# A graph layer on one core: gathered rows of two tables in separate buffers, and the order of a few steps around the start of the pair loop

## The chip, the cores and the metric

The kernel runs on one core of a Trainium2 chip. The metric is the device time of one execution in microseconds (us); the time before is the median of 9 runs. The profile comes from one further execution. In the text, PE is TensorE (PEld its weight loads), DVE is VectorE, ACT is ScalarE, POOL is GpSimd and SP is SyncE. L492 means line 492 of the kernel before.

## The reference, cut to what matters

```python
# 6250 nodes of 128 values, 100000 edges (src, dst) sorted by dst; hidden width 256
h = relu(concat(x[src], x[dst]) @ Wm1 + bm1)     # [100000, 256]
h = relu(h @ Wm2 + bm2)                          # [100000, 256]
messages = h @ Wm3 + bm3
agg = segment_sum(messages, dst) / clip(count_of_edges(dst), 1.0)
upd = relu(concat(x, agg) @ Wn1 + bn1) @ Wn2 + bn2
out = layernorm(x + (x + upd))                   # [6250, 128]
```

## The kernel before

**Two tables first.** The first product is split: `concat(x[src], x[dst]) @ Wm1` is a row of `A = x @ Wm1[:128]` plus a row of `B = x @ Wm1[128:]`. A prologue turns x by 13 blocks of 512 nodes (`turn`), multiplies (`products`, L258) and writes table A in float32 (`a_table`) and table B as three bfloat16 terms whose sum is the float32 value (`b_table`) to DRAM. B is computed five blocks behind A. Meanwhile small loads fetch weights (`weights`, whose loads are held back until a certain block is turned by a one-element VectorE copy into their targets), and the edges' indices are arranged: `srcT` holds the source of every edge, one column of 128 edges for each gather; `pbase`, `dloc` and `tilei` say to which window of 21 destinations each tile of 128 edges belongs.

The prologue also computes `x @ Wn1[:128]` into the space of x and of its transpose (`xu`): `x_part(b, ...)` does it for block b, two matmuls (L355) and two evacuations (L358 on ACT, L360 on DVE). Ten blocks are done in the prologue, block 9 (`X_FIRST`) after the first `first_layer`, block 10 at the end of the loop.

**The pair loop.** Edges go in groups of 512 (four tiles of 128), two groups to a pair, 98 pairs, written as a Python loop (L644) and so unrolled. The order of PE, DVE, ACT and POOL inside it is the order of the program text. One turn of the loop holds, for different pairs:

- `fetch` for the pair ahead: on POOL eight indirect DMAs (L492), each of which brings 128 rows of A (1 KB each) by the indices in `srcT`; on SP eight loads of 64 rows of B's terms (L498). All go into one tile `rows` of five parts, four for A and one, reread as bfloat16, for B; there are two such buffers, so the gathers of a pair wait for the first layer of the pair two before it.
- `destinations` for the pair ahead (L384, issued by ACT): the edges' destinations, spread over 64 partitions.
- `turned` and `add_up` for the pair three back: 12 transposes on PE (L584) into two banks, then eight small additions on DVE (L594) into the running sums `acc`.
- `make_hot`: DVE compares destinations with node numbers, giving the one-hot matrices `oht` (L516) and `oh` (L519).
- `first_layer`: on PE 32 transposes of A's rows (L533) into the PSUM tile `ph`, then 16 matmuls that add B's rows through `oht` (L540); on ACT four evacuations with bias and ReLU into `h1` (L546).
- `sums` for the pair two back: 16 matmul instructions (L565) into two banks, copied out by ACT (L573).
- `second_layer` for the pair before: 32 matmul instructions (L555) into four banks, evacuated by four DVE operations with the maximum against minus the bias (L557) into `h2s`.

`bank()` hands out four PSUM banks in turn, so a turn of the loop goes twice round the four: `turned` takes two, `sums` two, `second_layer` four. `turned` of the next turn therefore waits for the first two L557, and the third and fourth bank of `second_layer` wait for the two copies L573. The wait of POOL's first gather is for the last L540, because L540 is the last reader of the shared `rows` tile; before it, POOL also waits for the eight SP loads that last wrote that buffer.

```python
rows = ld.tile([P, 2, (GT + 1) * H], F32, name="rows", bufs=2)      # L487
ag = rows[:, i, :GT * H].rearrange("p (j h) -> p j h", j=GT)        # A's rows, L490
bw = rows[:, i, GT * H:].bitcast(BF16).rearrange(...)               # B's terms, L495
```

**After the loop** come a loop for windows that are too wide (its count is computed from the data), and the node stage over 15 stretches of nodes: mean of the messages, update, layer norm, store.

Of the kernel before, what the change touches and what calls it, by code (L numbers as in the profile page):

```python
# [27 lines left out]
def kernel(  # L28
# [121 lines left out]
    with tc.tile_pool(name="prep", bufs=1) as prep, tc.tile_pool(  # L150
# [34 lines left out]
            nc.gpsimd.dma_start(bu1, bn1.rearrange("(c p) -> p c", p=P))  # L185

        def weights(block):
            for t in (wu1, w3, w2):
                nc.vector.tensor_copy(t[:, 0, :1], xT[:, block * 4 * P:block * 4 * P + 1])
            nc.gpsimd.dma_start(nb2[:, 0, :], bm2.rearrange("(o h) -> o h", o=1).to_broadcast([P, H]))  # L190
            nc.sync.dma_start(wu1, wn1.rearrange("(k p) h -> p k h", p=P))
            nc.sync.dma_start(w3, wm3.rearrange("(k p) h -> p k h", p=P))
            nc.sync.dma_start(w2, wm2.rearrange("(k p) h -> p k h", p=P))

        nc.vector.memset(xT[:, N:], 0.0)

# [77 lines left out]
        def b_stores():  # L274
            while due:
                nc.sync.dma_start(*due.pop(0))
# [71 lines left out]
        def x_part(b, bank, engines):  # L348


            n0, n1 = 4 * b * P, min(4 * b * P + 4 * P, N)
            for c, eng in zip((1, 0), engines):
                pxu = bank().rearrange("p t h -> p (t h)")[:, :n1 - n0]
                i = 4 if b < BLOCKS - 1 else 1
                nc.tensor.matmul(pxu.rearrange("p (n i) -> p i n", i=i), wu1[:, 0, c * P:(c + 1) * P],  # L355
                                 xT[:, n0:n1].rearrange("p (i n) -> p i n", i=i), start=True, stop=True)
                if eng is nc.scalar:
                    nc.scalar.activation(xu[c][:, n0:n1], pxu, AF.Identity, bias=bu1[:, c:c + 1])  # L358
                else:
                    nc.vector.tensor_scalar(xu[c][:, n0:n1], pxu, bu1[:, c:c + 1], None, op0=ALU.add)  # L360
                yield

        def whole(steps):
            for _ in steps:
                pass
# [9 lines left out]
        def destinations(g, ng, dst_row):  # L375

            db = ld.tile([P, 2, 2 * P], I32, name="db", bufs=3)
            if isinstance(g, int) and g < 6:

                nc.vector.tensor_copy(db[:, 0, :1], srcT[:, 0, :1])  # L380
            for h in range(2):
                edges = dst_row[:, ds(g * GE, ng * GE)].rearrange("o (s e) -> o s e", s=ng)
                edges = edges[:, :, h * 2 * P:(h + 1) * 2 * P]
                nc.scalar.dma_start(db[h * NQ:(h + 1) * NQ, :ng, :], edges.to_broadcast([NQ, ng, 2 * P]))  # L384
            return [db[:, k, :] for k in range(ng)]
# [20 lines left out]
        for i in range(BLOCKS):  # L406
            if i in X_LOADS:
                load_x(*X_LOADS[i], behind=i)
                if X_LOADS[i][1] == BLOCKS - 1:
                    nc.sync.dma_start(x_sb[:N - NTF * P, NTF, :], x[NTF * P:, :])  # L410
            for n, t0 in enumerate(range(4 * i, min(4 * i + 4, NT), 2)):

                if n == (i == 0) and i + 1 < BLOCKS:
                    turn(4 * i + 4)
                a_table(t0)
            b_stores()
            for _ in range(min(len(blank), 3 if i < BEHIND else 1)):
                nc.gpsimd.memset(blank.pop(0), 0.0)
            if i == BEHIND + 1:
                weights(i)  # L420
            if i == INDICES:
                starts()
            if i - INDICES in (1, 2):
                columns(i - INDICES - 1)
                partition_bases(i - INDICES - 1)
            if i == BLOCKS - 1:
                nc.scalar.copy(tilei, base[0:1].rearrange("p r w -> p (r w)"))
                nc.gpsimd.tensor_scalar(nb2, nb2, -1.0, None, op0=ALU.mult)
            if i >= BEHIND:
                b_block(i - BEHIND)  # L430
            if BLOCKS - 3 <= i:
                early.append(destinations(2 * len(early), 2, dst_row))
        assert not blank
        behind = list(X_BEHIND)
        with tc.manual_schedule(engines={ENG.DVE}):
            for n, j in enumerate(range(BLOCKS - BEHIND, BLOCKS)):
                if n < 4:
                    whole(x_part(behind.pop(0), bank_pb, (nc.scalar, (nc.scalar, nc.vector)[n % 2])))
                b_block(j)
                b_stores()  # L440
            b_terms()
            b_stores()
        stores.close()


        turns.enter_context(tc.manual_schedule(engines={ENG.DVE}))
        for n, b in enumerate(behind):
            whole(x_part(b, bank_pb, (nc.vector if n >= len(behind) - 2 else nc.scalar, nc.vector)))
        pb3 = pp.tile([P, 1], F32, name="pb3", tag="pp")
        for c in range(HC):  # L450
            nc.tensor.matmul(pb3, w3[:, c, :], b2[:, c:c + 1], start=(c == 0), stop=(c == HC - 1))
        nc.vector.tensor_add(b23, b3, pb3)

# [10 lines left out]
    with edge, tc.tile_pool(name="wk", bufs=2) as wk, tc.tile_pool(  # L464
# [19 lines left out]
        def fetch(groups, queues):  # L484


            rows = ld.tile([P, 2, (GT + 1) * H], F32, name="rows", bufs=2)  # L487
            got = []
            for i, ((idx, firsts), queue) in enumerate(zip(groups, queues)):
                ag = rows[:, i, :GT * H].rearrange("p (j h) -> p j h", j=GT)  # L490
                for j in range(GT):
                    nc.gpsimd.indirect_dma_start(  # L492
                        out=ag[:, j, :], out_offset=None, in_=atab[:, :],
                        in_offset=bass.IndirectOffsetOnAxis(ap=idx[:, j:j + 1], axis=0))
                bw = rows[:, i, GT * H:].bitcast(BF16).rearrange("p (k h) -> p k h", k=2)  # L495
                for j, first in enumerate(firsts):
                    terms = btab[ds(first, WB + 1)].rearrange("n c h -> (n c) h")
                    queue.dma_start(bw[j // 2 * NQ:(j // 2 + 1) * NQ, j % 2, :], terms[:NQ])  # L498
                got.append((ag, bw))
            return got  # L500
# [23 lines left out]

        halves = [slice(h * NQ, (h + 1) * NQ) for h in range(2)]

        def first_layer(got, ohts, nts):
            ph = p1.tile([P, 2, 2, HC, 2 * P], F32, name="ph")
            for i, ((ag, bw), nt) in enumerate(zip(got, nts)):
                for c in range(HC):  # L530
                    for u in range(GT):
                        for h in range(nt // 2):
                            nc.tensor.matmul(ph[:, i, h, c, u * NQ:(u + 1) * NQ], ag[halves[h], u, c * P:(c + 1) * P],  # L533
                                             ident[halves[h], halves[h]], is_transpose=True,
                                             start=(c == 0 and u == 0), stop=False, skip_group_check=True)
            for i, ((ag, bw), nt) in enumerate(zip(got, nts)):
                for c in range(HC):
                    for k in range(2):
                        for h in range(nt // 2):
                            nc.tensor.matmul(ph[:, i, h, c, k * P:(k + 1) * P], bw[halves[h], k, c * P:(c + 1) * P],  # L540
                                             ohts[halves[h], i, k, :], start=False, stop=True, skip_group_check=True)
            h1 = wk.tile([P, 2, HC, GE], F32, name="h1")
            for i in reversed(range(len(nts))):
                nh = nts[i] // 2
                for c in range(HC):
                    nc.scalar.activation(h1[:, i, c, :nh * 2 * P].rearrange("p (h e) -> p h e", h=nh),  # L546
                                         ph[:, i, :nh, c, :], AF.Relu, bias=b1[:, c:c + 1])
            return h1

        def second_layer(h1, h2, nt):  # L550
# [93 lines left out]
        for i in range(NP + 4):  # L644
# [28 lines left out]
                    double((i - after) // 4, step)  # L673
            if p + 1 < NP:
                make_hot(p + 1)
            if p == 0:
                clear(3)
            if p < NP:
                s = st[p]
                s["h1"] = first_layer(s.pop("got"), s.pop("ohts"), s["nts"])  # L680
            if p == 0:
                whole(x_part(X_FIRST, bank, (nc.scalar, nc.vector)))
            if p - 2 == NP - 1:
                next(rest)
            if 0 <= p - 2 < NP:
# [269 lines left out]
```

## Time and profile before

| | |
|---|---|
| median of 9 runs | 1709.92 us (1701.01 to 1717.09) |
| the profiled execution: its own time, its span | 1717.37 us, 1715.2 us |
| mean granted clock of TensorE | 0.855 |
| busy: PE, PEld | 1343.8 us (78%), 1056.1 us |
| busy: DVE, ACT, POOL | 658.5, 380.6, 812.0 us |
| prologue, up to the first L533 | 87.8 us |
| pair loop, up to the node stage | from 87.8 to about 1642 us |
| node stage | about 73 us |
| window 400 to 1200 us | PE busy 617.3 of 800 us, POOL 381.7, DVE 282.3, ACT 148.6 |

The profile's page gives busy time by engine and by line; the waits say who stood for whom; the timeline gives single instructions in order. Matmuls are pipelined and their ends are modelled, so PE's busy share is an upper bound of its work. "remote" as the releaser of a wait means that the profile has no instruction that ended just then.

### The profile page before, as it was taken

The page shows a single profiled execution, that of the slowest core. Times are in us where ns is not written, and L with a number is a line of the kernel's source. Part 1 is how long each engine was busy: PE and PEld are TensorE (multiplying, and loading weights), DVE is VectorE, ACT ScalarE, POOL GpSimd, SP SyncE. Part 2 cuts the span into 40 slices and gives each one's busy share as a digit, 9 for nine tenths or more (in the row PEclk, how much of TensorE's full clock was granted, in tenths as well). Part 3 has the DMA queues.
Part 4 walks back from the last instruction along what each step waited for, and adds up shares of the span by engine and source line. Part 5 has one row for each costly group of instructions (what it writes and reads, how often), then busy time and mean ns, then how long its engine had stood idle before and what let it go on. Part 6 is the DMA issues. An engine that isn't in the chain of part 4 may idle for free. (4 is left out here: it accounts for less than half of the span.)

```text
span 1715.2 us, 32176 instructions
## 1 busy us (share of the span) xinstructions
PE 1343.8 (78%) x11222; PEld 1056.1 (62%) x11223; DVE 658.5 (38%) x2073; ACT 380.6 (22%) x768; POOL 812.0 (47%) x871
## 2 busy tenths in 40 slices
PE   9868778777777777777877877777788787777898
PEld 8456566566665655656656665666666566656656
DVE  5534323333332333333333333333233333333467
ACT  6512112212211211212211221221222122212235
POOL 7654454445445445445544544544544454445121
PEclk9888888888888888788888888878888888888899
DMA  8743344334334334334434433433433333333133
GB/s 295 271 117 110 98 111 113 105 104 117 106 99 123 106 94 122 105 93 123 116 87 114 114 89 101 111 88 98 110 99 98 102 107 101 98 103 108 38 111 111
DMA packets 167752, 193.67 MB, mean 113 GB/s; under 512 B 31074, under 2 KB 133428, under 8 KB 167572
## 3 DMA queue, kind: packets, MB, share of 16 engines
q0 software_dynamic: 38160, 103.75, 21.9%
q1 hardware_dynamic: 100640, 61.84, 12.3%
q10 hardware_dynamic: 28788, 26.01, 5.3%
q8 instruction: 89, 1.46, 0.4%
q14 instruction: 75, 0.61, 0.1%
HBM read 168.97 MB, written 22.88 MB: 112 GB/s over the span
## 5 line engine op out<-in xcount | busy, mean ns | idle before, releaser
L492 POOL DMA_INDIRECT rows<-atab,srcT x784 | 748.4, 955 | 800.0 <-PE ph L540 581.7
L555 PE MATMUL bank<-w,h 128*128 128x256 f32 x3128 | 710.5, 386 | 0.6 <-issue 0.4
L555 PEld LDWEIGHTS bank<-w,h 128*128 128x128 f32 x3128 | 593.8, 193 | 136.4 <-PE bank L565 57.9
L557 DVE TENSOR_TENSOR h<-bank,nb 128x512 f32<-128x512 f32 x391 | 254.8, 688 | 967.3 <-remote 474.4
L546 ACT ACTIVATE h<-ph,b 128x512 f32<-128x512 f32 x392 | 237.0, 688 | 1244.3 <-PE ph L540 1206.4
L584 PE MATMUL bank<-ident,part 64*128 64x64 f32 x1173 | 102.3, 289 | 328.8 <-DVE h L557 317.8
L584 PEld LDWEIGHTS bank<-ident,part 64*128 64x128 f32 x1173 | 73.0, 183 | 375.8 <-DVE h L557 338.3
L533 PE MATMUL ph<-ident,rows 64*128 64x64 f32 x3128 | 191.3, 300 | 15.8 <-issue 14.3
L533 PEld LDWEIGHTS ph<-ident,rows 64*128 64x128 f32 x3128 | 178.6, 209 | 19.6 <-issue 16.1
L594 DVE TENSOR_TENSOR acc<-acc,bank 128x63 f32 x782 | 171.7, 220 | 34.8 <-DVE acc L594 2.1
L565 PE MATMUL bank<-h,oh 128*32 128x257 f32 x1564 | 156.2, 536 | 0.2 <-ACT x_sb L358 0.2
L540 PE MATMUL ph<-oht,rows 64*128 64x128 bf16 x1564 | 110.2, 304 | 6.3 <-issue 5.5
L540 PEld LDWEIGHTS <-rows 64*128 64x128 bf16 x1564 | 94.3, 144 | 7.2 <-issue 7.2
L516 DVE TENSOR_SCALAR oht<-db,pbase 128x128 bf16<-128x128 int32 x392 | 94.8, 288 | 0.3
L565 PEld LDWEIGHTS bank<-h,oh 128*32 128x32 f32 x1564 | 52.3, 143 | 57.0 <-issue 29.5
L573 ACT COPY part<-bank 128x257 f32<-128x257 f32 x196 | 66.6, 400 | 11.9 <-PE bank L565 9.0
L519 DVE TENSOR_TENSOR oh<-iota_n,dloc 128x128 f32<-128x128 f32 x196 | 55.4, 283 | 0.0
L778 POOL TENSOR_TENSOR agg<-total,rc 128x512 f32<-128x512 f32 (+2 forms) x15 | 15.9, 1071 | 81.3 <-DVE total L775 78.1
L258 PE MATMUL pbt<-w,xT 128*128 128x256 f32 x196 | 46.7, 382 | 0.9 <-DVE rest L285 0.6
L258 PEld LDWEIGHTS pbt<-w,xT 128*128 128x128 f32 x196 | 35.7, 190 | 8.4 <-DVE rest L285 2.4
L355 PE MATMUL pxu<-xT,wu 128*128 128x512 f32 x40 | 21.4, 673 | 7.6 <-ACT x_sb L358 7.6
L815 PEld LDWEIGHTS pot<-wu,u 128*128 128x128 f32 x192 | 23.6, 192 | 4.8 <-issue 4.3
(134 smaller groups left out, 421.4 us busy)
## 6 DMA issues: line engine op xcount, KB each, us to landing
rows<-btab SPq DMA_DIRECT2D x778, 32.0 KB
db<-in_dst_dram ACTq DMA_DIRECT2D x194, 128.0 KB
rows<-atab,srcT POOLq DMA_INDIRECT x784
btab<-acc SPq DMA_DIRECT2D x24, 384.0 KB
atab<-at SPq DMA_DIRECT2D x24, 256.0 KB
xd<-in_x_dram SPq DMA_DIRECT2D x12, 256.0 KB
x2tab<-xd SPq DMA_DIRECT2D x12, 256.0 KB
x_sb<-in_x_dram SPq DMA_DIRECT2D x5, 512.0 KB
```

Of the source, the lines that this page charges most:

```text
L258: nc.tensor.matmul(pbt[:, a, :], xT[:, (t0 + a) * P:(t0 + a + 1) * P], w1[:, k, :], start=True, stop=True)
L492: nc.gpsimd.indirect_dma_start(out=ag[:, j, :], out_offset=None, in_=atab[:, :], in_offset=bass.IndirectOffsetOnAxis(ap=idx[:, j:j + 1], a ...
L516: nc.vector.tensor_scalar(ohts[:n, i, k, :], db[:n, k * P:(k + 1) * P], pb_cols[:n, k:k + 1], None, op0=ALU.is_equal)
L533: nc.tensor.matmul(ph[:, i, h, c, u * NQ:(u + 1) * NQ], ag[halves[h], u, c * P:(c + 1) * P], ident[halves[h], halves[h]], is_transpose=Tru ...
L540: nc.tensor.matmul(ph[:, i, h, c, k * P:(k + 1) * P], bw[halves[h], k, c * P:(c + 1) * P], ohts[halves[h], i, k, :], start=False, stop=Tru ...
L546: nc.scalar.activation(h1[:, i, c, :nh * 2 * P].rearrange("p (h e) -> p h e", h=nh), ph[:, i, :nh, c, :], AF.Relu, bias=b1[:, c:c + 1])
L555: nc.tensor.matmul(ph2[:, j - j0, :], h1[:, c, j * P:(j + 1) * P], w2[:, c, :], start=(c == 0), stop=(c == HC - 1))
L557: nc.vector.tensor_tensor(h2[:, j0:j0 + 2, :H], ph2, nb2.to_broadcast([P, 2, H]), op=ALU.max)
L565: nc.tensor.matmul(pg[j * WN:(j + 1) * WN, :H + 1], oh[:, j, :], h2[:, j, :], start=True, stop=True, skip_group_check=True)
L573: nc.scalar.copy(part[:nt * WN, i], pg[:nt * WN, :H + 1])
L584: nc.tensor.matmul(pts[h][:, i, c, :], rows, ident[halves[h], halves[h]], is_transpose=True, start=True, stop=True, skip_group_check=True)
L594: nc.vector.tensor_add(window, window, pts[h][:, i, :, k:k + WB])
```

## The change

It does five things.

1. `fetch` takes two tiles instead of one: `arows` for the gathered rows of A, `brows` for B's terms, two buffers each, the same bytes in all.
2. The load of `w2` (256 KB) leaves `weights` and is issued by SP after the last store of B.
3. Only the first pair's destinations are loaded three blocks before the end of the table stage; the second pair's are issued after the prologue's last `x_part`, and the third pair's in the loop.
4. The product of `w3` and `b2` (`pb3`) stands two `x_part`s earlier.
5. `x_part` of block 9 moves inside the first `first_layer`, between its transposes and its B matmuls, with both evacuations on DVE; in that first layer, the first group's two evacuations go to DVE as well. The clearing of three slots moves behind it.

```diff
         def weights(block):
-            for t in (wu1, w3, w2):
+            for t in (wu1, w3):
...
-            nc.sync.dma_start(w2, wm2.rearrange("(k p) h -> p k h", p=P))
...
-            if isinstance(g, int) and g < 6:
+            if isinstance(g, int) and g < 2:
...
-            if BLOCKS - 3 <= i:
-                early.append(destinations(2 * len(early), 2, dst_row))
+            if i == BLOCKS - 3:
+                early.append(destinations(0, 2, dst_row))
...
             b_terms()
             b_stores()
+        nc.sync.dma_start(w2, wm2.rearrange("(k p) h -> p k h", p=P))
...
         for n, b in enumerate(behind):
+            if n == 2:
+                pb3 = pp.tile([P, 1], F32, name="pb3", tag="pp")
+                for c in range(HC):
+                    nc.tensor.matmul(pb3, w3[:, c, :], b2[:, c:c + 1], start=(c == 0), stop=(c == HC - 1))
+                nc.vector.tensor_add(b23, b3, pb3)
             whole(x_part(b, bank_pb, (nc.vector if n >= len(behind) - 2 else nc.scalar, nc.vector)))
-        pb3 = pp.tile([P, 1], F32, name="pb3", tag="pp")
-        for c in range(HC):
-            nc.tensor.matmul(pb3, w3[:, c, :], b2[:, c:c + 1], start=(c == 0), stop=(c == HC - 1))
-        nc.vector.tensor_add(b23, b3, pb3)
+        early.append(destinations(2, 2, dst_row))
...
-            rows = ld.tile([P, 2, (GT + 1) * H], F32, name="rows", bufs=2)
+            arows = ld.tile([P, 2, GT * H], F32, name="arows", bufs=2)
+            brows = ld.tile([P, 2, 2, H], BF16, name="brows", bufs=2)
...
-                ag = rows[:, i, :GT * H].rearrange("p (j h) -> p j h", j=GT)
+                ag = arows[:, i].rearrange("p (j h) -> p j h", j=GT)
...
-                bw = rows[:, i, GT * H:].bitcast(BF16).rearrange("p (k h) -> p k h", k=2)
+                bw = brows[:, i]
...
-        def first_layer(got, ohts, nts):
+        def first_layer(got, ohts, nts, between=None):
...
+            if between is not None:
+                whole(between)
             for i, ((ag, bw), nt) in enumerate(zip(got, nts)):
...
+                    if between is not None and i == 0:
+                        nc.vector.tensor_scalar(to, ph[:, i, :nh, c, :], b1[:, c:c + 1], 0.0,
+                                                op0=ALU.add, op1=ALU.max)
+                    else:
+                        nc.scalar.activation(to, ph[:, i, :nh, c, :], AF.Relu, bias=b1[:, c:c + 1])
...
-            if p == 0:
-                clear(3)
             if p < NP:
                 s = st[p]
-                s["h1"] = first_layer(s.pop("got"), s.pop("ohts"), s["nts"])
+                between = x_part(X_FIRST, bank, (nc.vector, nc.vector)) if p == 0 else None
+                s["h1"] = first_layer(s.pop("got"), s.pop("ohts"), s["nts"], between)
             if p == 0:
-                whole(x_part(X_FIRST, bank, (nc.scalar, nc.vector)))
+                clear(3)
```

In the instruction order of the changed kernel POOL's first gather of a pair waits for the last transpose L533 of the pair two before, and for no load of SP; SP's first load of a pair still waits for the last L540.

More of the change, by code (lines that the diff above doesn't have):

```diff
@@ L545, in first_layer @@
                 for c in range(HC):
-                    nc.scalar.activation(h1[:, i, c, :nh * 2 * P].rearrange("p (h e) -> p h e", h=nh),
-                                         ph[:, i, :nh, c, :], AF.Relu, bias=b1[:, c:c + 1])
+                    to = h1[:, i, c, :nh * 2 * P].rearrange("p (h e) -> p h e", h=nh)
+                    if between is not None and i == 0:
[3 more added lines that the diff above has]
+                        nc.scalar.activation(to, ph[:, i, :nh, c, :], AF.Relu, bias=b1[:, c:c + 1])
             return h1
@@ L675 @@
                 make_hot(p + 1)
+            if p < NP:
+                s = st[p]
+                between = x_part(X_FIRST, bank, (nc.vector, nc.vector)) if p == 0 else None
+                s["h1"] = first_layer(s.pop("got"), s.pop("ohts"), s["nts"], between)
             if p == 0:
                 clear(3)
-            if p < NP:
-                s = st[p]
-                s["h1"] = first_layer(s.pop("got"), s.pop("ohts"), s["nts"])
-            if p == 0:
-                whole(x_part(X_FIRST, bank, (nc.scalar, nc.vector)))
             if p - 2 == NP - 1:
```

## The prediction

> **What bounds the kernel now.** I read the page's list of costly groups first, then the waits of the whole run, then the timeline of one pair in mid-loop, and last a pair that began its gathers unusually early. From the page (busy us, mean ns of one, idle before it and its releaser):
>
> ```profile
> L492 POOL DMA_INDIRECT rows<-atab,srcT x784 | 748.4, 955 | 800.0 <-PE ph L540 581.7
> L584 PE MATMUL bank<-ident,part 64*128 64x64 f32 x1173 | 102.3, 289 | 328.8 <-DVE h L557 317.8
> ```
>
> POOL stands 581.7 us before its gathers, for the B matmuls of the first layer. PE, the busiest engine, stands 317.8 us before the transposes L584, for DVE. The waits (total us, times, longest) carry that back:
>
> ```profile
> DVE h L557 <- remote: 474.4, 101, 10.3
> DVE h L557 <- PE bank L555: 373.6, 83, 7.9
> PE bank L584 <- DVE h L557: 317.8, 104, 4.8
> POOL rows L492 <- PE ph L540: 581.7, 95, 13.1
> ```
>
> So the odd wait is that of L557: half of it ends at nothing that the profile knows. The timeline of one pair (start, length):
>
> ```profile
> 814.88 1.89 DVE L557 TENSOR_TENSOR h<-bank,nb 128x512 f32<-128x512 f32 x3 [5.08 <-remote]
> 815.62 0.90 PE L584 MATMUL bank<-ident,part 64*128 64x64 f32 x11 [4.11 <-DVE h L557]
> 816.22 2.01 PE L533 MATMUL ph<-ident,rows 64*128 64x64 f32 x32
> 817.92 1.16 PE L540 MATMUL ph<-oht,rows 64*128 64x128 bf16 x16
> 819.06 0.28 DVE L519 TENSOR_TENSOR oh<-iota_n,dloc 128x128 f32<-128x128 f32 x1
> 819.36 1.00 POOL L492 DMA_INDIRECT rows<-atab,srcT  x1 [6.66 <-PE ph L540]
> 820.86 7.17 PE L555 MATMUL bank<-w,h 128*128 128x256 f32 x32
> ...
> 828.18 0.94 POOL L492 DMA_INDIRECT rows<-atab,srcT  x1 [0.30 <-issue]
> 831.24 1.89 DVE L557 TENSOR_TENSOR h<-bank,nb 128x512 f32<-128x512 f32 x3 [6.75 <-remote]
> 832.59 2.01 PE L533 MATMUL ph<-ident,rows 64*128 64x64 f32 x32
> ```
>
> PE has issued all of L555 by 828.0, yet three L557 start back to back at 831.24, which is 11.9 us after the first gather (819.36) and 2.1 us after the last one ended on POOL (828.18 + 0.94). In the trace's packets the gathers' data end 0.6 us before that. The records of PE's counter show the same: it is advanced promptly until some 0.8 us after the first gather, with delay from 1.3 us on, and the last three advances of L555 arrive together 11.7 to 12.3 us after it. I read this as: while the gathers run, PE's signals reach DVE late, and the end of the gathers releases them. A loop follows: gathers start, 11.9 us, L557, L584, L533, L540, gathers start. Its period is 16.37 us here (816.22 to 832.59), 15.9 in the mean of 90 pairs.
>
> A pair whose gathers began early tests that reading:
>
> ```profile
> 1495.39 1.16 PE L533 MATMUL ph<-ident,rows 64*128 64x64 f32 x31
> 1497.27 0.95 POOL L492 DMA_INDIRECT rows<-atab,srcT  x1 [4.15 <-PE ph L540]
> 1500.82 0.37 ACT L573 COPY part<-bank 128x257 f32<-128x257 f32 x1 [1.03 <-PE bank L555]
> 1506.06 0.94 POOL L492 DMA_INDIRECT rows<-atab,srcT  x1 [0.30 <-issue]
> 1509.11 2.48 DVE L557 TENSOR_TENSOR h<-bank,nb 128x512 f32<-128x512 f32 x4 [9.65 <-remote]
> ```
>
> The gathers start 1.9 us after the transposes' start instead of 3.1, and L557 follows again 11.84 us later. But all four L557 now stand behind the release, and the second copy L573 came late.
>
> **The change, part by part.** *Separate tiles.* POOL's first gather waits for the last L533 and no longer for L540 and SP's loads. From the pair above: the ends of L533 (816.22 + 2.01) and L540 (817.92 + 1.16) lie 0.85 us apart. Between PE's signal and the gather lie, in the trace, four waits of POOL for the SP loads, 0.05 to 0.09 us each; without them about 0.20 us go. So the gathers start 1.05 us sooner, 2.1 instead of 3.14 us after L533's start. With the loop above this is 1.05 us a pair, in the 95 pairs where POOL waits for L540: 100 us at most. SP's loads of B still start after L540; they have a whole turn before they are read, and a slower SP costs nothing.
>
> What is given back. First, behind the earlier gathers lie three more signals of PE (L540 and the two sums L565). In before, the second signal to fall into the delayed time (that of L555's first bank) arrived 4 to 12 us after the first gather, mostly near 6. Now this place belongs to the second sum. Its copy L573 frees the fourth bank of L555, due 7.8 us after the gather. Up to there nothing is lost; held until the release it costs 1.5 us (worked out with the slower rival below). I take that in a tenth of the pairs, 0.15 (bounds 0 and 0.45). Second, L557's first operation then comes more often only at the release, which puts one more L557 (0.60 us from start to start) before L584: in about 13 of 90 pairs before, I guess half after, 0.20 us (bounds 0 and 0.50). Net 1.05 - 0.35 = 0.70 us a pair (bounds 0.10 and 1.05), times 95: 66.5 us.
>
> A rule against this. The earlier gathers share their time with L519 and L594 on DVE. The row at hand: the gather at 819.36 ran beside an L519 and took 1.00 us, against a mean of 0.955, so at most 0.06 us a pair; that lies inside the bounds above and I take nothing for it. The Trainium skill (SBUF — State Buffer, "Who interferes with whom") says that a VectorE instruction with two SBUF inputs, as L519 is, and a GpSimd instruction that reads SBUF exclude each other for the whole instruction. By that, an estimate from the page, two L519 of 0.28 us could hold the gathers up 0.56 us a pair, and the sum would be 53 us less.
>
> *The clock.* PE's granted clock falls with its long stand (us, then busy PE, PEld, DVE, ACT, POOL, then the clock):
>
> ```profile
> 810.80:814.20 3.40, 0.72 (x4) 0.25 (x2) 0.00 (x0) 0.00 (x0) 1.59 (x2) 0.96 0.43 128
> 814.20:817.60 3.40, 1.98 (x37) 1.98 (x38) 2.62 (x7) 0.00 (x0) 0.00 (x0) 0.50 0.00 0
> ```
>
> With a clock of 0.50 L533 takes 2.01 us, in the early pair at full clock 1.2. The stand will shrink from 3.9 to about 2.9 us. A pair that had 2.73 us of it (954.48 to 957.20) still ran the next L533 in 2.01, so I take no gain; the bound is 0.7 us in half of the pairs. The Trainium skill (TensorE: Matmul & The Clock Gate, "Why this matters for your kernels") warns of stands of PE over about 3 us; by that a stand of 2.9 us would keep the full clock in most pairs, an estimate of up to 66 us more.
>
> *Start of the loop.* `w2` (256 KB) and four destination loads (128 KB each) leave the stretch in which the DMA engines are full (330 to 379 GB/s between 20 and 60 us): 0.77 MB by 0.33 MB/us, up to 2.3 us, if the gathers (first at 56.4) really wait for those bytes. `w2` is needed by the first L555 at 101, 30 us after B's last store; its cover is the 16 first gathers, and without it the load would cost its 1 to 2 us. SP issues it ahead of the first pair's loads, which are needed 17 us later: nothing. Block 9's two products (0.87 us at full clock, up to 1.98 in the row at 89.47) now stand before the first L540 and no longer after it: the second pair's first layer was stuck behind the gathers anyway (its L540 took from 93 to 101). Two evacuations on DVE instead of ACT save up to 1.2 us there, `pb3` and `clear` move behind other work at nothing. I take 2 us gained (bounds 5 gained, 4 lost).
>
> **The sum.** 66.5 + 2 = 68.5, rounded 69 us: 1717.4 - 69 = 1648 for the profiled execution. That execution lies 7.5 us above the median of 1709.9; I take the same difference off the median: **1641 us**. Its own range is 1609 (1.05 us a pair) to 1700 (0.10).
>
> **The rivals.** *No change:* the release at 11.9 us is set by something that does not follow the gathers, and L557 keeps its place. For it: the profile names no releaser. Against it: 11.8 to 12.0 us in pairs whose gathers start 1.9 to 6.0 us after L533. Time: 1710 - 2 = 1708.
>
> *Slower:* the signal of the second sum is held to the release in every pair. Its place is the wait of L555's fourth bank for L573. Then copy and signal take 0.6 us, the bank's eight instructions 1.75, L584 starts 2.1 + 11.9 + 0.6 + 1.75 = 16.3 us after L533, and the period is 16.8 instead of the 15.3 of a pair that gives nothing back, or the 16.4 of before: 0.4 x 95 = 38 us more, 1746; with the first sum's signal held too, another 1.75 us a pair, 1912. It decides from the point where the copy starts later than about 10.7 us after the gather. For it: the early pair, where L573 waited 1.0 us for a signal due 2.9 us sooner. Against it: it still came 3.5 us after the gather.
>
> *More:* nothing is given back and the clock stays full in half of the pairs: (1.05 + 0.35) x 95 + 2 = 135, 1575.
>
> **How the numbers follow.** Forecast 0.70, no change 0.07, slower 0.13, more 0.10. The forecast is the likeliest, so 1641. The range from 1600 to 1702 leaves out the slower case and most of "more". A measurement of this kernel tells 0.3% (5 us) from no change; half of the no-change case lies beyond that on the fast side through the start: faster 0.83, same 0.04, slower 0.13.
>
> **What would show it.** In the profile after: POOL's first gather released by L533 and starting about 2.1 us after it; three or four L557 again 11.9 us behind it; PE's stand before L584 near 3 us, 230 to 260 us in total; a period near 15.2 to 15.6 us. It is wrong if L557 no longer follows the gathers at a fixed distance, if PE now stands before L555's third or fourth bank, or if the period does not move while the gathers do.

## The result, and the profile after

The changed kernel took 1820.34 us in the median of 20 runs (1794.05 to 1838.45), the kernel before 1715.77 us in 62 (1698.01 to 1733.77): ratio 1.058, 95% interval 1.055 to 1.060. It is slower; 1641 was predicted, in a range of 1600 to 1702. The ratio leaves out executions over 1.5% above the fastest of their kernel, so it lies a little under that of the two medians. The profiled execution of the changed kernel has a span of 1806.8 us, against 1715.2 before. L533 is now L536, L540 L545, L546 L556, L555 L564, L557 L566, L565 L574, L573 L582, L584 L593, and the gathers L492 are L495. The lines shift again in the kernels of the experiments; there the names of the tiles tell which instruction a row is (`ph<-ident` the transposes, `ph<-oht` the B matmuls, `bank<-w,h` the second layer, `part` the copies of the sums, `h<-bank` the maxima).

The costly groups of the changed kernel (busy us, mean ns of one, idle time before it and its releaser):

```profile
L495 POOL DMA_INDIRECT arows<-atab,srcT x784 | 750.7, 958 | 887.2 <-PE ph L536 665.6
L564 PE MATMUL bank<-w,h 128*128 128x256 f32 x3128 | 824.7, 421 | 315.7 <-ACT part L582 238.5
L593 PE MATMUL bank<-ident,part 64*128 64x64 f32 x1173 | 87.3, 279 | 114.9 <-DVE h L566 114.1
```

POOL is released by the transposes L536, as the change means it to be. PE's stand ahead of the transposes L593 has fallen from 317.8 to 114.1 us. But PE now stands 238.5 us ahead of L564 for ScalarE's copies, where it stood 0.6 us in all before, and L564 itself is busy 824.7 us where L555 was 710.5. The row of before:

```profile
L555 PE MATMUL bank<-w,h 128*128 128x256 f32 x3128 | 710.5, 386 | 0.6 <-issue 0.4
```

The waits (total us, times, longest) of the changed kernel:

```profile
DVE h L566 <- remote: 807.0, 85, 10.8
POOL arows L495 <- PE ph L536: 665.6, 94, 11.3
ACT part L582 <- remote: 413.6, 76, 9.2
PE bank L564 <- ACT part L582: 238.5, 61, 6.0
```

The third line is new (1.2 us in all before): ScalarE's copies of the sums now end their wait at nothing that the profile knows, as VectorE's maxima did before. The fourth line is the price. One pair of the changed kernel in the timeline (start, length):

```profile
801.78 1.16 PE L536 MATMUL ph<-ident,arows 64*128 64x64 f32 x32
803.22 0.94 POOL L495 DMA_INDIRECT arows<-atab,srcT  x1 [8.24 <-PE ph L536]
804.32 3.72 PE L564 MATMUL bank<-w,h 128*128 128x256 f32 x16
...
808.59 0.38 ACT L582 COPY part<-bank 128x257 f32<-128x257 f32 x1 [2.68 <-PE bank L564]
809.02 1.99 PE L564 MATMUL bank<-w,h 128*128 128x256 f32 x8 [0.98 <-ACT part L582]
811.98 0.95 POOL L495 DMA_INDIRECT arows<-atab,srcT  x1 [0.30 <-issue]
815.11 0.37 ACT L582 COPY part<-bank 128x257 f32<-128x257 f32 x1 [6.14 <-remote]
815.20 1.89 DVE L566 TENSOR_TENSOR h<-bank,nb 128x512 f32<-128x512 f32 x3 [8.81 <-remote]
815.54 3.78 PE L564 MATMUL bank<-w,h 128*128 128x256 f32 x8 [4.52 <-ACT part L582]
819.25 0.90 PE L593 MATMUL bank<-ident,part 64*128 64x64 f32 x12
```

The gathers start 1.44 us after the transposes and not 3.14. PE is done with the sums at 804.39, but their second copy is made at 815.11, 11.9 us after the first gather, at the release. The fourth bank of L564 stands 4.52 us for that copy, and then its eight instructions take 3.78 us. The stretches of that stand and of the bank (length, busy PE, PEld, DVE, ACT, POOL, then the granted clock, the DMA engines' share and GB/s) show why:

```profile
811.02:815.54 4.52, 0.00 (x1) 0.01 (x1) 0.34 (x1) 0.37 (x1) 1.61 (x2) 0.91 0.39 109
815.54:819.25 3.71, 3.71 (x9) 2.53 (x9) 1.55 (x3) 0.00 (x0) 0.00 (x0) 0.50 0.58 169
```

The bank runs at a clock of 0.50, so 3.78 us stand where the third bank's eight took 1.99.

Over all pairs whose turn holds eight gathers (87 before, 93 after), the instructions' starts in the two traces give this, in us, means:

| | gathers start after the transposes | next transposes after the first gather | period |
|---|---|---|---|
| before | 3.14 | 12.79 | 15.93 |
| after, all 93 | 1.86 | 15.05 | 16.91 |
| after, 37 pairs with the second copy up to 9 us after the first gather | 2.17 | 13.74 | 15.90 |
| after, 41 pairs with it over 10.9 us after, at the release | 1.56 | 16.53 | 18.09 |

(The 15 pairs between the last two rows have a period of 16.2.) So the gathers do start 1.28 us sooner, and 2.26 us are given back.

### The profile page after: what moved, and what is told of

Read it like the earlier page. It is cut to its first block, busy times and chain, and to the rows that moved or that the text cites. A ratio compares the mean times of both kernels' runs of the same rounds, so it can differ in the third digit from the quotient of the medians.

```text
span 1806.8 us, 31499 instructions
## 1 busy us (share of the span) xinstructions
PE 1351.0 (75%) x11222; PEld 1031.9 (57%) x11223; DVE 659.6 (37%) x2073; ACT 393.7 (22%) x765; POOL 814.3 (45%) x871
## 5 line engine op out<-in xcount | busy, mean ns | idle before, releaser
L495 POOL DMA_INDIRECT arows<-atab,srcT x784 | 750.7, 958 | 887.2 <-PE ph L536 665.6
L564 PE MATMUL bank<-w,h 128*128 128x256 f32 x3128 | 824.7, 421 | 315.7 <-ACT part L582 238.5
L564 PEld LDWEIGHTS bank<-w,h 128*128 128x128 f32 x3128 | 633.9, 209 | 496.4 <-ACT part L582 265.1
L566 DVE TENSOR_TENSOR h<-bank,nb 128x512 f32<-128x512 f32 x391 | 248.6, 686 | 1041.1 <-remote 807.0
L556 ACT ACTIVATE h<-ph,b 128x512 f32<-128x512 f32 x390 | 235.9, 687 | 715.2 <-PE ph L545 469.4
L582 ACT COPY part<-bank 128x257 f32<-128x257 f32 x196 | 73.7, 378 | 622.2 <-remote 413.6
L593 PE MATMUL bank<-ident,part 64*128 64x64 f32 x1173 | 87.3, 279 | 114.9 <-DVE h L566 114.1
L593 PEld LDWEIGHTS bank<-ident,part 64*128 64x128 f32 x1173 | 64.4, 177 | 172.8 <-DVE h L566 144.9
L536 PE MATMUL ph<-ident,arows 64*128 64x64 f32 x3128 | 154.8, 267 | 5.9 <-issue 5.1
L536 PEld LDWEIGHTS ph<-ident,arows 64*128 64x128 f32 x3128 | 146.5, 181 | 7.5 <-issue 5.8
L574 PE MATMUL bank<-h,oh 128*32 128x257 f32 x1564 | 117.3, 421 | 0.2 <-ACT x_sb L357 0.2
L519 DVE TENSOR_SCALAR oht<-db,pbase 128x128 bf16<-128x128 int32 x392 | 96.6, 300 | 0.4 <-issue 0.2
L545 PE MATMUL ph<-oht,brows 64*128 64x128 bf16 x1564 | 78.8, 246 | 3.1 <-issue 3.1
L545 PEld LDWEIGHTS <-brows 64*128 64x128 bf16 x1564 | 66.2, 113 | 4.6 <-issue 4.6
L574 PEld LDWEIGHTS bank<-h,oh 128*32 128x32 f32 x1564 | 43.6, 117 | 35.7 <-issue 6.6
L781 PE MATMUL pmt<-acc,w 128*128 128x512 f32 (+2 forms) x60 | 24.8, 549 | 2.6 <-DVEq L710 2.6
```

The lines of the kernel that those rows point to most:

```text
L495: nc.gpsimd.indirect_dma_start(out=ag[:, j, :], out_offset=None, in_=atab[:, :], in_offset=bass.IndirectOffsetOnAxis(ap=idx[:, j:j + 1], a ...
L519: nc.vector.tensor_scalar(ohts[:n, i, k, :], db[:n, k * P:(k + 1) * P], pb_cols[:n, k:k + 1], None, op0=ALU.is_equal)
L556: nc.scalar.activation(to, ph[:, i, :nh, c, :], AF.Relu, bias=b1[:, c:c + 1])
L564: nc.tensor.matmul(ph2[:, j - j0, :], h1[:, c, j * P:(j + 1) * P], w2[:, c, :], start=(c == 0), stop=(c == HC - 1))
L566: nc.vector.tensor_tensor(h2[:, j0:j0 + 2, :H], ph2, nb2.to_broadcast([P, 2, H]), op=ALU.max)
L574: nc.tensor.matmul(pg[j * WN:(j + 1) * WN, :H + 1], oh[:, j, :], h2[:, j, :], start=True, stop=True, skip_group_check=True)
```

## The experiments

The theory: while gathers run, signals of PE arrive late, and the earlier gathers catch one more of them, that of the second sum. The rivals: the loss comes from the other parts of the change; or the late signals have nothing to do with the gathers.

**The parts apart, the sums first, no gathers.** Four kernels, on one chip:

```
tiles only:   before, with  arows = ld.tile(...)  and  brows = ld.tile(...)  for  rows
rest only:    after, with one  rows  tile again
sums first:   after, with  part_of(summed(p - 2), ...)  moved between L536 and L545 of first_layer
no gathers:   after, from the third pair on
  - nc.gpsimd.indirect_dma_start(...)        + nc.gpsimd.memset(arows[:, :, :1], 0.0)
```

In the last one A's rows stay those of the first two pairs.

> The kernel before with the two tiles apart and nothing else. Theory 1 (the loop's loss comes from the gathers' earlier start: PE's signal of the second sum comes when the gathers already run, is held until about 11.9 us after the first of them, and the fourth bank of the second layer stands for the copy): all of the loss is here, 1810 to 1835 us, the second sum's copy later than 10.9 us behind the first gather in about 40 of 92 pairs, the fourth bank late in most. Theory 2 (the loss comes from the other parts: w2 and the destinations loaded late, the ninth block inside the first first-layer): near the kernel before, 1712 to 1722 us, a pair's period 15.8 us.

> The change without the tiles apart: one tile holds both tables' rows again, all the other parts stay. Theory 1: the loop is that of the kernel before, so 1708 to 1716 us: the start's 2 to 3 us gained and nothing lost; the gathers start about 3.1 us behind the first transpose of the pair. Theory 2: near the changed kernel, 1805 to 1830 us.

> The changed kernel with the sums of the pair before moved from behind the first layer's B matmuls to ahead of them, so that their signals are given 1 us after the transposes instead of 2 us after. Theory 1: the second copy comes 1.0 to 3.5 us behind the first gather and the fourth bank no longer stands for it; the B matmuls' signal is now the one given last before the hold. If it passes as the second sum's did in the kernel before (by 3.5 us), a pair takes 15.0 to 15.7 us and the run 1640 to 1700 us; if it is caught, the activations of the first layer come at the release and the run is over 1850 us. Theory 2: the order of these matmuls means nothing, 1800 to 1830 us.

> The changed kernel without its gathers from the third pair on (the loop's rows of the first table are those of the first pairs; GpSimd writes one column into the tile instead, so that all other waits stay). Theory 1: with no gathers PE's signals are prompt, idle time behind remote work is gone from VectorE and ScalarE, and a pair takes PE's own work of 11.6 to 12.6 us: 1380 to 1500 us. Rival (the waits have to do with PE and ScalarE themselves, the gathers only fill the time): a pair stays over 15 us, over 1700 us.

All four missed, for a reason in none of the theories: on this chip the kernel before took 1150.15 us in the median of 19 runs. Tiles only took 1149.61 us (ratio 1.000, 0.999 to 1.002), rest only 1151.77 (1.002, 1.001 to 1.003), the sums first 1163.19 (1.012, 1.009 to 1.015), no gathers 1153.14. The changed kernel itself, on another chip:

> The changed kernel itself once more. In the first four runs the kernel before took 1150 us instead of 1716 us: PE was busy 99% of the span, and no signal of PE was late while gathers ran. Theory 1 (the loss of 5.8% comes only where PE's signals are held): where the kernel before takes 1150 us, the changed kernel takes 1148 to 1155 us; where the kernel before takes 1716 us, 1800 to 1830 us. Theory 2 (the loss is work that the change adds): the changed kernel is slower by some per cent also where the kernel before takes 1150 us, 1180 to 1250 us.

1152.93 us against 1150.87 (1.002, 1.001 to 1.003), as theory 1 expected; the parts that the change adds cost almost nothing there. Its page shows another kernel, though the program is the same:

```profile
PE 1133.4 (99%) x11222; PEld 913.8 (79%) x11223; DVE 684.2 (59%) x2073; ACT 377.4 (33%) x765; POOL 810.7 (70%) x871
L564 PE MATMUL bank<-w,h 128*128 128x256 f32 x3128 | 702.4, 383 | 0.7 <-DVE acc L603 0.6
L582 ACT COPY part<-bank 128x257 f32<-128x257 f32 x196 | 65.3, 401 | 7.1 <-PE bank L574 7.1
```

PE is busy 99% of the span and never stands in the loop, no wait ends at "remote", and each pair takes 10.06 us with every tile and order but the sums first (10.17). The gathers run as before, 953 ns each. So there are chips on which PE's signals are prompt while gathers run, and there this change moves nothing in the loop. I call the others late chips: those on which the kernel before takes some 1660 to 1735 us, as in the runs of the result. Over the experiments four chips were prompt and three late; two chips came up twice, and were prompt both times. What makes a chip late, no run shows.

The small loss on prompt chips is at the start of the loop. PE's instructions there, first with the tiles apart only, then in the changed kernel:

```profile
79.27 1.29 PE L541 MATMUL ph<-oht,brows 64*128 64x128 bf16 x15 [3.12 <-DMA brows<-btab]
84.12 1.21 PE L534 MATMUL ph<-ident,arows 64*128 64x64 f32 x32
85.70 7.17 PE L556 MATMUL bank<-w,h 128*128 128x256 f32 x32
```

```profile
81.94 0.34 PE L545 MATMUL ph<-oht,brows 64*128 64x128 bf16 x5 [1.09 <-DMA brows<-btab]
85.33 1.97 PE L536 MATMUL ph<-ident,arows 64*128 64x64 f32 x32 [3.05 <-DVE h L553]
88.08 8.24 PE L564 MATMUL bank<-w,h 128*128 128x256 f32 x32
```

B's first rows are used up 1.7 us later (82.28 against 80.56), the ninth block no longer fills the time after them, and PE stands 3.05 us for VectorE's ReLU L553; then transposes and matmuls run slower. The third first layer starts at 96.25 us instead of 92.81, 3.4 us later.

Tiles only and no gathers were run again on chips that turned out prompt, with 1148.98 (ratio 1.000) and 1152.33 us, and a third time with 1149.77 (1.000) and 1152.8 us. With that third time went a kernel whose gathers wait for the second copy:

```
after, in fetch, ahead of the gathers:
  + nc.gpsimd.tensor_copy(held, last_part.pop()[:, 1, :1])
```

> The changed kernel, and GpSimd reads one column of the second copy of the sums (of the turn that runs) ahead of its gathers: the tiles stay apart, but the gathers wait until that copy is made, some 2 to 3 us later in the turn. Theory 1 (the loss comes because the gathers start before the second sum's signal has gone out): on a chip with late signals the copy is no longer held, the fourth bank no longer stands, and a pair takes 15.3 to 16.2 us, 1660 to 1740 us in all against about 1820 us for the changed kernel. Rival (the loss has another cause, and later gathers only add their delay): a pair takes 1 to 2 us more than in the changed kernel, 1900 to 2000 us. On a chip with prompt signals both expect about 1153 us, PE being busy throughout.

1156.09 us (1.005, 1.004 to 1.007), 3 us over the 1153 expected.

**Held by hand.** Four kernels with the late signal imitated by a wait that is in the program:

```
+ gate = wk.tile([P, 90], F32, ...);  10 x  nc.gpsimd.memset(gate, 0.0)     behind the gathers
+ nc.vector.tensor_copy(seen[:, :1], gate[:, :1])    ahead of the second (first) maximum of the pair
+ nc.scalar.copy(seen[:, 1:], gate[:, :1])           ahead of the second copy of the sums (last kernel)
```

For these reads the next pair's `fetch` also moves, in all four, from the start of its turn to ahead of the second layer of the turn before (in the last one to between the two copies).

> A model of late signals on chips where they are prompt. The kernel before, with work added from the fifth pair on: behind its eight gathers GpSimd writes a small tile ten times, up to about 11.5 us after the first gather, and VectorE reads that tile ahead of the second of the pair's four second-layer maxima. So three of the four come only after the gathers, as in the profile of before where PE's signals were late. Theory 1 (the loop gathers, release, maxima, turning, first layer, gathers sets the time when signals are late): a pair takes 15.3 to 16.3 us as it did in that profile, against 10.06 us without the wait, so 1630 to 1720 us. Rival (late signals cost in other ways too, the wait for the gathers alone is not the loop): a pair stays under 14 us, below 1510 us.

> The same added wait in the kernel with the two tiles apart and nothing else. Theory 1, the gain that was predicted: the gathers start about 1.05 us sooner in each turn and everything behind them too, so 0.8 to 1.3 us a pair less than with one tile, 75 to 120 us in 91 pairs. Rival (the earlier gathers gain nothing even where nothing else is held): the same time within 20 us.

> The tiles apart, and the read of the small tile ahead of the first maximum instead of the second: all four come after the gathers, as in 90 of 92 pairs of the changed kernel's late profile. Theory 1: one maximum more behind the release, 0.5 to 0.7 us a pair more than with three held, 45 to 65 us. Rival (the first maximum has no part in the loop): no difference.

> As the run before, and ScalarE too reads the small tile ahead of its second copy of the sums, so that this copy comes after the gathers, as in 40 of 92 pairs of the changed kernel's late profile. Theory 1: the second layer's fourth bank stands until the copy, 4 matmul pairs of it at full or half clock come behind the release, and a pair takes 1.5 to 3.5 us more than in the run before, 140 to 320 us. Rival (the fourth bank has slack): no difference.

The chip was a late one: the kernel before took 1715.18 us there, so the added wait stands beside real late signals. One tile: 1785.44 us, over the 1630 to 1720 expected; a pair takes 16.61, and the second maximum now comes over 10.9 us after the first gather in all of 91 pairs, in the profile of before in 70 of 91. Tiles apart: 1817.02 (1811.38 to 1822.66), 32 us more, where 75 to 120 less were expected. The waits of the kernel with the tiles apart:

```profile
DVE h L568 <- remote: 862.2, 88, 11.2
ACT part L586 <- remote: 416.3, 75, 9.1
PE bank L564 <- ACT part L586: 220.8, 45, 6.9
```

In the kernel with one tile no copy is released so, and the second copy comes 2.37 us after the first gather in the median; here it is at the release in 39 of 93 pairs. Between these two only the tiles differ. Holding the first maximum too changed nothing that two runs show (1824.39, 1810.99 to 1837.78, against the expected 45 to 65 more): with the tiles apart it was held already, in 91 of 93 pairs. Holding the second copy in every pair gave 1984.37, 160 us more, as expected: the fourth bank has no slack for it.

**Stages in one kernel.** As chips differ, the next kernel holds five variants in one run:

> The changed kernel with its 98 pairs in five stages, so that one profile compares them on one chip. Pairs 4 to 23: GpSimd writes a column of the second table's rows ahead of its gathers, which makes them wait for the B matmuls as with one tile. Pairs 24 to 47: the changed kernel. Pairs 48 to 67: the gathers wait for the turn's second copy of the sums, the tiles apart. Pairs 68 to 81: the sums and their copies ahead of the B matmuls. Pairs 82 to 95: no gathers (their rows stay those of earlier pairs). Theory 1 on a chip with late signals, mean period of a pair: 15.6 to 16.2, 16.6 to 17.4, 15.2 to 16.2, 14.8 to 16.5 (or over 18, if the B matmuls' signal is then the one held), 10.1 to 11.5 us; second copies at the release only in the second stage. Theory 2 (the loss is from the other parts, which all stages have): the first three stages within 0.4 us of one another, near 17 us. Theory 3 (the signals are late whatever GpSimd does): the last stage over 14 us. On a chip with prompt signals 10.1 to 10.2 us in every stage, about 1155 us in all.

The chip was late (the kernel before: 1662.8 us). This one took 1662.1, without the gathers of 14 pairs. Its five stages in windows (length, then as above; 17, 20, 18, 11 and 13 pairs):

```profile
156.38:439.47 283.09, 215.38 (x1840) 169.54 (x1840) 94.64 (x311) 50.56 (x102) 131.51 (x153) 0.81 0.38 103
503.20:833.23 330.03, 240.37 (x2165) 185.41 (x2165) 112.67 (x367) 62.69 (x120) 153.08 (x160) 0.88 0.37 104
861.46:1162.48 301.02, 237.55 (x1950) 179.29 (x1948) 104.54 (x328) 53.33 (x108) 139.89 (x162) 0.82 0.34 98
1213.94:1380.18 166.24, 133.12 (x1193) 104.11 (x1192) 59.55 (x198) 34.90 (x66) 84.08 (x88) 0.87 0.38 105
1391.91:1522.70 130.79, 130.79 (x1411) 107.40 (x1408) 74.54 (x235) 38.51 (x78) 1.33 (x13) 1.00 0.19 54
```

Divided by their pairs: 16.65, 16.50, 16.72, 15.11 and 10.06 us. The last stage speaks against theory 3: without gathers PE is busy all the time at a clock of 1.00, on a late chip too. But the first three stages lie within 0.22 us of one another, near 17 us, which is what theory 2 expected: this run does not part theories 1 and 2.

The third stage was expected at 15.2 to 16.2 and failed. There the gathers start 10.6 us (median) after the transposes and run into the next pair's first layer, and it is the transposes themselves that come slowly:

```profile
960.88 0.84 PE L547 MATMUL ph<-ident,arows 64*128 64x64 f32 x21
966.85 0.58 PE L547 MATMUL ph<-ident,arows 64*128 64x64 f32 x5 [0.44 <-issue]
967.13 1.16 PE L557 MATMUL ph<-oht,brows 64*128 64x128 bf16 x16
968.38 2.42 ACT L568 ACTIVATE h<-ph,b 128x512 f32<-128x512 f32 x4 [14.00 <-PE ph L557]
```

The 32 transposes take 5.45 us there in the median, 1.29 in the second stage; ScalarE's evacuations follow the last B matmul after 0.1 us in all 18 pairs, so no late signal is seen at that place. What slows the transposes the profile does not say. The first stage did not separate from the second; no second copy was held in it (1.9 to 2.3 us after the first gather), but its extra instruction of GpSimd let the gathers start at 3.64 us, not at 3.14, in most pairs. So it was made again without one:

```
after, in three kinds of stages, 15 pairs each, twice
kind 1:  the last of the 32 transposes moved behind the 16 B matmuls     kind 2:  as it is
kind 3:  part_of(summed(p - 2), ...)  between the transposes and the B matmuls
```

(A pair has 32 transposes; the 64 in the expectation is a slip.)

> The changed kernel in three kinds of stages that take turns, 15 pairs each, twice over: one of the pair's 64 transposes behind the B matmuls, so that the gathers wait for these as with one tile, with no instruction added (kind 1); the changed kernel (kind 2); the sums and their copies ahead of the B matmuls (kind 3). Nothing is left out of the computation. On a chip with late signals, mean period of a pair by theory 1: kind 1 15.6 to 16.1 us, kind 2 16.5 to 17.2, kind 3 14.9 to 15.5; second copies at the release and a standing fourth bank in kind 2 alone. Theory 2 (the loss is in the other parts, which all kinds have): kinds 1 and 2 within 0.3 us. On a chip with prompt signals 10.06, 10.06 and 10.17 us.

> The same kernel a third time, the chips of the two runs before having prompt signals. On a chip with late signals, mean period of a pair by theory 1: kind 1 (the gathers wait for the B matmuls) 15.6 to 16.1 us, kind 2 (the changed kernel) 16.5 to 17.2, kind 3 (the sums first) 14.9 to 15.5; theory 2 (the loss is in the parts that all kinds have): kinds 1 and 2 within 0.3 us. On a chip with prompt signals 1155 us again.

Two runs of it were on prompt chips (10.06, 10.06 and 10.17 us by kind; 1155.62 and 1162.22 us). The third was on a late one (before 1707.72 us, this 1739.04). Windows of the stages of kinds 1, 2, 3, 1, 2, 3, of 14, 13, 13, 12, 13 and 13 pairs:

```profile
144.55:365.65 221.10, 170.29 (x1518) 137.98 (x1516) 77.58 (x255) 41.47 (x84) 106.97 (x112) 0.85 0.40 109
382.59:604.85 222.26, 160.61 (x1408) 124.90 (x1408) 73.55 (x239) 40.80 (x78) 98.90 (x104) 0.84 0.37 103
637.87:842.11 204.24, 164.60 (x1408) 126.89 (x1408) 71.97 (x238) 41.25 (x78) 99.26 (x104) 0.83 0.39 109
874.37:1066.74 192.37, 145.71 (x1300) 118.78 (x1300) 66.92 (x220) 35.55 (x72) 91.57 (x96) 0.83 0.38 103
1113.45:1339.00 225.55, 160.50 (x1410) 122.94 (x1408) 71.32 (x235) 41.13 (x78) 99.13 (x104) 0.85 0.32 92
1370.03:1571.53 201.50, 157.30 (x1410) 122.59 (x1409) 70.27 (x235) 41.25 (x78) 99.26 (x104) 0.87 0.37 103
```

| kind | period, first and second stage | gathers after the transposes | next transposes after the first gather | second copy at the release |
|---|---|---|---|---|
| 1, gathers behind the B matmuls | 15.79, 16.03 | 3.10, 3.16 | 12.70, 12.87 | 0 of 26 |
| 2, the changed kernel | 17.10, 17.35 | 1.81, 1.70 | 15.29, 15.65 | 14 of 26 |
| 3, the sums first | 15.71, 15.50 | 2.20, 2.07 | 13.51, 13.43 | 0 of 26 |

Kind 1 came as expected; kind 2 came once within its range and once 0.15 us above it, kind 3 once at the upper end of its own and once 0.2 us above. Kinds 1 and 2 differ in one transpose's place, and with it in when the gathers start: 1.3 us a pair, or 125 us in 95 pairs. That is no less than the whole loss of 92 us, and kind 1 has the period of the kernel before (15.93); theory 2, by which the two lie within 0.3 us, falls. Kind 3 takes the loss back, but little more: it lies 0.1 and 0.5 us under kind 1, and on prompt chips its order costs 1.2%. No version here beats the kernel before on both sorts of chip.

The two kinds in the timeline, second copy and release:

```profile
241.87 0.94 POOL L495 DMA_INDIRECT arows<-atab,srcT  x1 [5.92 <-PE ph L541]
244.25 0.41 ACT L595 COPY part<-bank 128x257 f32<-128x257 f32 x1
253.66 1.89 DVE L579 TENSOR_TENSOR h<-bank,nb 128x512 f32<-128x512 f32 x3 [4.34 <-remote]
...
551.39 0.94 POOL L495 DMA_INDIRECT arows<-atab,srcT  x1 [8.44 <-PE ph L541]
563.43 0.37 ACT L595 COPY part<-bank 128x257 f32<-128x257 f32 x1 [6.18 <-remote]
563.52 1.89 DVE L579 TENSOR_TENSOR h<-bank,nb 128x512 f32<-128x512 f32 x3 [9.92 <-remote]
563.85 3.59 PE L577 MATMUL bank<-w,h 128*128 128x256 f32 x8 [4.56 <-ACT part L595]
```

In kind 1 the second copy is made 2.4 us after the first gather and the release comes 11.8 us after it. In kind 2 copy, maxima and fourth bank all come at the release, 12.0 us after it.

## Why the prediction was wrong, point by point

- **The reading held, on late chips.** The release follows the gathers: over 91 pairs in each trace it comes 11.8 us after the first of them in the median before (in a tenth of the pairs 10.9 or less) and 12.0 us after the change. Without gathers it is gone (10.06 us a pair). That PE's signals are late on some chips only could not be read from one profile.
- **Earlier gathers: near in size, in part by luck.** 1.05 us sooner was worked out, all of it from the shorter wait; 1.28 was measured. From the end of the last transpose to the first gather 1.10 us became 0.28, which is 0.82. The other 0.46 us come from the transposes, which take 1.60 us instead of 2.06 in the mean, a gain of clock that was put at nothing.
- **What is given back: the step that failed.** It was put at 0.35 us a pair and bounded at 0.95; it is 2.26. Its two terms were mis-sized. First, the maxima: I guessed that L557's first operation would come at the release in half of the pairs; it does in 91 of 93 (before, counted in the same way, in 4 of 87; the prediction had 13 of 90). The price of one more maximum was right: from the release to the next transposes go 1.84 us with four behind it (35 pairs with copies in time) against 1.28 with three before, 0.56 more against the 0.60 worked out. The release itself also lies 0.2 us later in those pairs. Together, even in the 37 pairs whose copies came in time, the next transposes start 0.95 us later after the first gather than before (13.74 against 12.79), which alone cancels the 0.97 us that those pairs' gathers start sooner. This was put at 0.20, at most 0.50. Second, the second sum: I took it as held in a tenth of the pairs; it was at the release in 41 of 93, and 15 more came 9 to 10.9 us after the gather. This makes the other 1.31 us (2.26 less 0.95), put at 0.15. PE then stands before L555's fourth bank, 238.5 us in all, which the prediction had named as a sign that it is wrong.
- **The ground of that guess.** From the row of L555's first bank, whose signal had come mostly near 6 us, I gave the second sum's signal the same delay, and slack until 7.8. It came 9.86 us after the gather in the median. A signal's place in the order did not tell how late it comes.
- **The slower rival was the right mechanism, at 0.13, in 41 of 93 pairs.** It put a held pair at a period of 16.8; held pairs take 18.09. It counted the fourth bank at 1.75 us up to L584; behind stands of 4.5 us it ran at about half clock, 3.7 and 3.5 us in the two pairs shown, and took 2.9 to 3.8 us in all held pairs. The rest of its sum holds, by the kind-2 pair above: 1.52 to the gathers, 12.04 to the copy, 0.42 to the bank, 3.52 for it, 0.42 to the next transposes, 17.92.
- **The clock.** I took no gain; there was one, and a larger loss, and neither was in the sum. In the held pairs the transposes take 1.21 us in the median, against 2.01 before; in the pairs with copies in time they still take 2.01. All L533 are busy 191.3 us before and 154.8 after. Against this L555's 710.5 us became 824.7. The Trainium skill (TensorE: Matmul & The Clock Gate, "Why this matters for your kernels") warns of gaps of PE over about 3 us; the 4.52 us gap followed by a clock of 0.50 agrees. The stand of 2.73 us before, after which the transposes took 2.01 us, shows that a shorter one can cost the clock too.
- **The SBUF rule.** The 0.56 us a pair worked out from the page did not show: a gather takes 958 ns against 955 before, 0.02 us in eight. Something of it is there: gathers that run beside an L519 for 0.05 us or more take 0.99 to 1.00 us in both traces, the others 0.95. That is some 0.05 us each, not the 0.28 of an L519.
- **Start of the loop.** 2 us gained were predicted. In the late profile the first transposes start at 85.14 instead of 87.80, 2.7 us sooner, and those of the third pair at 109.21 instead of 111.53; on prompt chips they start 0.7 us later and the third first layer 3.4 us later.
- **The sum by what was measured.** (2.26 - 1.28) x 95 = 93 us, less 2.7 at the start: 90. The spans of the same two traces differ by 91.6.

## What to carry to other kernels

When a trace shows signals that arrive late while something runs, starting that something sooner does not only shift the loop: list, in order, every signal that now falls behind its start, and price each as held to the release, its consumer's slack and the clock behind the stand included. A mean period split at one event, here the first gather, shows at once which side gains and which pays. And run the kernel before again on more than one chip before the cause is sought: here the same program took 1807 or 1151 us of span, bound once by the loop through gathers and maxima and once by PE alone.

## What the hardware showed

- One program, two speeds by chip: 1806.8 and 1150.6 us of span for the changed kernel, a difference of 16.9 to 10.1 us a pair. In the late profile the maxima and copies waited up to 10.8 us for matmuls that had long ended by the profile; on the prompt ones such waits ended with PE's instructions.
- On a late chip a pair without gathers took 10.06 us, the same as on prompt chips with gathers. So the gathers are needed for the lateness, as far as 13 pairs of one run show, and not enough for it. Whether it is GpSimd's issue or the rows' traffic that delays the signals was not tried.
- The Trainium skill (Perfetto Trace Analysis, "Tensor Engine Instruction (MATMUL, LD_WEIGHTS)") puts the spreading of a matmul's semaphore update after the end that the profiler reports, and gives no length. Here the waits that the profile ends at "remote" last up to 10.8 us in the late profile of the changed kernel; whether it is this spreading that is late, no run shows.
- Order within the turn decides whose signal is late. With the sums first (kind 3) their copies came 1.7 us after the gather, and the evacuations of the first layer, signalled next, 1.9 and 2.7 us (medians of the two stages) after the last B matmul, where kind 2 has 0.1:

```profile
703.10 0.38 ACT L595 COPY part<-bank 128x257 f32<-128x257 f32 x1 [9.98 <-PE bank L587]
703.74 0.62 PE L556 MATMUL ph<-oht,brows 64*128 64x128 bf16 x16
708.06 0.69 ACT L569 ACTIVATE h<-ph,b 128x512 f32<-128x512 f32 x1 [3.80 <-PE bank L577]
```
